# A two-layer 2D state-space block: near sums, their exponentials and DVE's near powers moved by one step in the first layer's scan

## The chip, the cores and the metric

The kernel runs on one NeuronCore of a Trainium2 chip, as one launch. The metric is the device time of that launch in microseconds (us). The time of a kernel is the median of its runs.

The engines go by short names: PE (TensorE, the matrix products; PEld is its loading of weights), DVE (VectorE), ACT (ScalarE), POOL (GpSimd) and SP (SyncE, which here issues nearly all DMAs). Each engine works through its own instructions in program order. An instruction that waits holds up everything behind it on its engine.

## The reference, cut to what matters

The input is a batch of 4 images of 64x64 positions with 192 channels. Two layers of a selective state-space model (four scan directions, 384 inner channels, 16 states) are added to it one after the other. Only the first layer's scan is touched by the change:

```
x = x + layer0(groupnorm(x))
x = x + layer1(groupnorm(x))

# layer0, for each of 4 directions, over the 4096 positions in that direction's order
delta = softplus(dts @ W_dt + b)            # 384 channels
h = exp(delta * A) * h + delta * B * u      # h: 384 x 16 states; A = -exp(A_log)
y = sum over the 16 states of h * C         # then + u * D
```

In this data `A` is -1, -2, ..., -16 (up to a common factor) for the 16 states. So the decay for state n is the n-th power of one decay, and the powers can be made one from the other by a product.

## The kernel before, in words

**Blocks and rounds.** The scan of the first layer goes over the 4096 positions in blocks of 30, which makes 137 rounds. A round treats one block of all four directions and all four images at once, in tiles of 128 partitions (two halves of 64 rows; each half has two directions of 30 rows, and 4 rows for the state carried in) and 1536 columns (4 images of 384 channels). Within a round there are 16 steps, one for each state, from state 16 down to state 1. So there are 2192 steps s, each belonging to round s // 16.

**One step.** For step s the kernel needs a tile x(s) of 128 x 1536, made as x(s) = x(s-1) * f, with f the exponential of the running sum of delta; the first of a round is dtu * g instead, with g the 16th power at once. This is `grown` (line 1063). Its columns are shared out: DVE makes the first 512 ("near"; line 1069 for the first of a round, line 1073 for the others), POOL the other 1024 ("far"). Into rows 60 to 63 of each half a DMA then writes the state carried over from the round before (`carry_in`, line 1018, DMA at line 1024). `mix` (line 1075, matrix products at line 1079) multiplies x(s) by a masked matrix b and adds the result to two accumulators in PSUM, j = 0 and 1, eight products each in the profile. After that `weigh` (lines 1084 and 1090; line 962 in the last step of a round) multiplies the accumulators by fd, on DVE, so that the next state's mix can add to them. In odd steps `keep_end` (line 1029) first copies both accumulators on ACT to the tile sx. From sx come two DMAs (`shrink`, tile small), a product on POOL (`settle`, line 1042) with an exponential from ACT (`decay`, line 1039), and the DMA `carry_out`, which stores the states for the next round. In even steps `outer` (line 1053) makes the outer products of B and C on PE, with 8 rows, and `cut_b` (line 1061) masks them on DVE.

So there is a chain: mix(s) on PE, in odd steps the copy on ACT, weigh(s) on DVE, mix(s+1) on PE.

**The order is written out by hand.** A loop over s (lines 1095 to 1131) emits for every s, engine by engine, the instructions of that turn. The offsets say how far ahead of the mix each piece is made. With AHEAD = 6 (line 1000), in the turn of step s:

- SP: shrink(s-1), carry_out(s-5), carry_in(s+4), then planned DMAs
- ACT: the copies of step s if s is odd, decay(s-2), then planned work
- POOL: grown(s+6), settle(s-4), then planned work
- DVE: weigh(s), grown(s+6), cut_b(s+2) if s is even, then planned work
- PE: mix(s+1), planned work, outer(s+4) if s is even

"Planned" work is what a round needs once: its deltas, sums and exponentials. `Round.steps` (line 974) lists it with an offset from the round's first step and an engine. An offset of -7 is the ninth step of the round before, counted from 0 (16 - 7 = 9). All of these matrix products go through one PSUM tile p, which has a single buffer, so each new product into p waits until the one before it has been read. In steps 5 to 14 of each round this tile is used for the next round, and from step 11 on for the one after that:

- step 8: `sums_d(1)` (line 922, products at line 845), read in step 9 by `keep_sums` (line 929, ACT, tile fd)
- step 9: `sums_near` (line 913), one product of 128 x 512, the running sums of the near columns
- step 10: `first_near` (line 916) and `fall_near` (line 920) on ACT read it. The first writes g of the near columns back into p, the second writes f of the near columns to another PSUM tile, f0. DVE's grown for the next round's first step reads g from p (line 1069)
- step 10: a repeated `sums_d(0)` whose result nobody reads (a filler product on PE); two more of these stand in steps 12 and 14
- step 11: `v(0)` (line 854; at line 845 with 26 rows), read in step 12 by `parts` (lines 862 and 863, ACT)
- step 13 and 14: the same for `v(1)` and its parts

`spread` (line 837, ACT) stands in every step; it prepares the tiles cs that outer reads. On SP, a round's results are stored in step 6 (`store_y`), after POOL has added the old ones in step 5 (`add_old`, line 965).

The x tiles have 7 buffers, f0 and p one each, b three.

Of the kernel before, what the change touches and what calls it, by code (L numbers as in the profile page):

```python
# [578 lines left out]
class FirstLayer(Stage):  # L579
# [182 lines left out]
    def scans(self):  # L762
        nc, tc = self.tc.nc, self.tc
        with ExitStack() as ctx:
# [44 lines left out]
            class Round:  # L809
# [164 lines left out]
                def steps(self):  # L974

                    s = lambda f, *a: (lambda: f(*a))
                    r = [(-30, "sp", self.load_xd), (-20, "sp", self.load_u), (-12, "sp", self.load_bc)]
                    for i in range(NS // PART):
                        r += [(PART * i - 8 + b, "act", s(self.spread, i, b)) for b in range(NB)]
                    for j in range(2):  # L980
                        r += [(2 * j - 21, "pe", s(self.v, j)), (2 * j - 20, "act", s(self.parts, j))]
                        r += [(2 * j - 19, "act", s(self.exp, j))]
                        r += [(2 * j - 13, "dve", s(self.times_u, j)), (2 * j - 13, "act", s(self.keep_dt, j))]
                        r += [(2 * j - 10, "pe", s(self.sums_d, j)), (2 * j - 9, "act", s(self.keep_sums, j))]
                    r += [(at, "pe", s(self.delta, 0, i)) for i, at in enumerate((-17, -16, -15, -14))]
                    r += [(at, "pe", s(self.delta, 1, i)) for i, at in enumerate((-13, -13, -12, -12))]
                    r += [(-16, "act", self.plus), (-15, "pool", self.rounded), (-14, "act", self.log)]
                    for i, at in ((1, -10), (2, -8)):
                        r += [(at - 1, "pe", s(self.sums_far, i))]
                        r += [(at, "act", s(self.first_far, i)), (at, "act", s(self.fall_far, i))]  # L990
                    r += [(-7, "pe", self.sums_near), (-6, "act", self.first_near), (-6, "act", self.fall_near)]
                    r += [(-4, "sp", self.keep_total), (-2, "act", self.log_total), (-1, "dve", self.test)]
                    r += [(10, "sp", self.load_y), (NS + 5, "pool", self.add_old), (NS + 6, "sp", self.store_y)]
                    r += [(at, "pe", s(self.sums_d, 0)) for at in (-6, -4, -2)]
                    return r

            w_dt, one, shift, zeros, late = self.w_dt, self.one, self.shift, self.zeros, self.late
# [2 lines left out]
            AHEAD = 6  # L1000
# [7 lines left out]
            def planned(s, engine):  # L1008
                for f in plan.get((s, engine), []):
                    f()  # L1010
# [7 lines left out]
            def carry_in(s):  # L1018
                n = state(s)
                m = (n - 1) // 2  # L1020
                v = carry[:, n % 2, m : m + 2].rearrange("c m q r f -> r (m q) c f")
                for r in range(2):
                    to = xs[s][r * HALF + 2 * RW : (r + 1) * HALF].rearrange("q (c f) -> q c f", c=2)
                    nc.sync.dma_start(to, v[r])

            def keep_end(s, j):
                if j == 0:
                    sxs[s] = p3.tile([128, W], F32, name="sx")
                nc.scalar.copy(paired(sxs[s], j), accs[j][:, :, :DI])  # L1029

            def shrink(s):
                small[s] = p3.tile([128, SMALL], F32, name="small")
                for c in range(2):
                    narrow(small[s], sxs[s], c)

            def decay(s):
                back[s] = p3.tile([128, SMALL], F32, name="back")
                n = state(s)
                nc.scalar.activation(back[s], of(s).tot, AF.Exp, bias=late[:, n // 2 : n // 2 + 1], scale=float(n))  # L1039

            def settle(s):
                nc.gpsimd.tensor_tensor(back[s], back[s], small[s], ALU.mult)  # L1042

            def carry_out(s):
                nc.sync.dma_start(carry_of(carry, (state(s) - 1) // 2), back[s])

            def outer(s):
                outs[s] = ps_o.tile([128, LC], F32, name="o")
                cs, p = of(s).cs[s % NS // PART], of(s).r % 2
                for h in range(2):  # L1050
                    n = state(s) - 1 - h
                    at = slice(h * NB * HALF, (h + 1) * NB * HALF)
                    nc.tensor.matmul(  # L1053
                        outs[s][:, at], at_b[p][:, n, :], cs[:, n % PART].rearrange("q b l -> q (b l)"),
                        start=True, stop=True, skip_group_check=True,
                    )

            def cut_b(s):
                bs[s] = p_b.tile([128, 2, NB, HALF], F32, name="b")
                o = outs[s].rearrange("p (h b l) -> p h b l", h=2, b=NB)  # L1060
                nc.vector.tensor_tensor(bs[s], o, bc(masks, 2, NB), ALU.mult)  # L1061

            def grown(s, engine):
                it = of(s)
                if s not in xs:
                    xs[s] = p_x.tile([128, W], F32, name="x")
                if s % NS == 0:
                    part, g = (slice(0, LC), it.m[:, 1, :]) if engine is nc.vector else (slice(LC, W), it.g)
                    engine.tensor_tensor(xs[s][:, part], it.dtu[:, part], g, ALU.mult)  # L1069
                    return  # L1070
                part = slice(0, LC) if engine is nc.vector else slice(LC, W)
                f = it.f0 if engine is nc.vector else it.f
                engine.tensor_tensor(xs[s][:, part], xs[s - 1][:, part], f, ALU.mult)  # L1073

            def mix(s, j):
                for r in range(2):
                    for c in range(2):
                        b = 2 * c + j
                        nc.tensor.matmul(  # L1079
                            accs[j][half(c), r, :DI], bs[s - s % 2][half(r), s % 2, b, :], xs[s][half(r), cols(b)],  # L1080
                            start=s % NS == 0, stop=state(s) == 1, skip_group_check=True,
                        )

            def weigh(s, j):
                n = state(s)
                if n == 1:
                    of(s).end_y(j)
                    return
                acc = accs[j][:, :, :DI]
                nc.vector.tensor_tensor(acc, acc, paired(of(s).fd, j), ALU.mult)  # L1090

            engines = {e.engine for e in (nc.tensor, nc.scalar, nc.vector, nc.gpsimd, nc.sync)}
            with tc.manual_schedule(engines=engines):
                tc.keep_in_program_order(nc.scalar.preload_act_table_set("natural_log_exp_and_others"))
                for s in range(-LEAD, N + 8):
                    on = lambda q: 0 <= q < N
                    pair = lambda q: on(q) and state(q) % 2 == 1
                    if pair(s - 1):
                        shrink(s - 1)
                    if pair(s - 5):  # L1100
                        carry_out(s - 5)
                    if on(s + AHEAD - 2):
                        carry_in(s + AHEAD - 2)
                    planned(s, "sp")
                    if pair(s):
                        for j in range(2):
                            keep_end(s, j)
                    if pair(s - 2):
                        decay(s - 2)
                    planned(s, "act")  # L1110
                    if on(s + AHEAD):
                        grown(s + AHEAD, nc.gpsimd)
                    if pair(s - 4):
                        settle(s - 4)
                    planned(s, "pool")
                    if on(s):
                        for j in range(2):
                            weigh(s, j)
                    if on(s + AHEAD):
                        grown(s + AHEAD, nc.vector)  # L1120
                    if on(s + 2) and s % 2 == 0:
                        cut_b(s + 2)
                    planned(s, "dve")
                    for j in range(2):
                        if on(s + 1):
                            mix(s + 1, j)
                    planned(s, "pe")
                    if on(s + 4) and s % 2 == 0:
                        outer(s + 4)
# [719 lines left out]
```

## Time and profile before

| | us |
|---|---|
| median of 3 runs | 9214.46 |
| lowest and highest | 9201.74, 9224.96 |
| the profiled execution, its own time | 9238.58 |
| its span, first to last instruction | 9236.7 |
| mean granted TensorE clock | 0.938 |

The profile is of one execution, 24 us above the median. The span has three stages: projections up to 711 us, the first layer's scan to 7469 us, and the rest (the end of the first layer, and the second layer) to 9237 us.

A row of a group or timeline gives the line of the code, the engine, the operation, the tile written and the tiles read, and the time. In brackets stands how long the engine sat idle just before, and what the profile takes as the releaser of that wait; "issue" means that it names none. Consecutive equal instructions of an engine are merged into one row (x2 and so on). The granted clock is the share of full speed that PE was given.

### The profile page before, as it was taken

What the parts mean: (1) busy time and instruction counts of PE and PEld (TensorE: products, weight loads), DVE (VectorE), ACT (ScalarE), POOL (GpSimd) and SP (SyncE); (2) the same over time, 40 slices, a digit from 0 to 9 for tenths busy, and PEclk for the clock granted to TensorE, in tenths of its full rate; (3) what the DMA queues carried; (4) which work ended last, traced back from release to release, by engine and by line L of the source; (5) the groups of instructions that cost most, each with busy time, mean ns of one, the idle gap of its engine ahead of it and who ended that gap; (6) DMA issues with size and microseconds to landing.
All of it is one profiled execution on the core that took longest, in us unless ns stands there. A gap on an engine that the chain in (4) does not pass through costs nothing. (4 is left out here: it accounts for less than half of the span.)

```text
span 9236.7 us, 194062 instructions
## 1 busy us (share of the span) xinstructions
PE 8325.8 (90%) x64280; PEld 3607.3 (39%) x64280; DVE 7548.9 (82%) x10238; ACT 6071.9 (66%) x10104; POOL 6605.4 (72%) x3814
## 2 busy tenths in 40 slices
PE   8989999999999999999999999999999945887668
PEld 4433333333333333333333333333333324543457
DVE  3428999999899899898899999999999954796756
ACT  3336676776667667666677767766767745675668
POOL 0008999999999999889999999999999952001460
PEclk9989999999999999999999999999999977887788
DMA  6652322322322322223333333333333379433458
GB/s 186 208 175 65 77 72 72 77 73 71 76 73 74 74 73 74 73 72 81 84 78 81 84 78 81 84 80 79 84 81 80 83 183 249 139 126 121 159 136 292
DMA packets 952264, 971.21 MB, mean 105 GB/s; under 512 B 550176, under 2 KB 802733, under 8 KB 950369
## 3 DMA queue, kind: packets, MB, share of 16 engines
q1 hardware_dynamic: 946192, 951.97, 37.9%
q0 software_dynamic: 5056, 6.66, 0.5%
q8 instruction: 521, 8.54, 0.4%
q14 instruction: 495, 4.05, 0.1%
HBM read 521.83 MB, written 375.80 MB: 97 GB/s over the span
## 5 line engine op out<-in xcount | busy, mean ns | idle before, releaser
L1073 POOL TENSOR_TENSOR x<-x,f 128x1024 f32<-128x1024 f32 x2055 | 4864.3, 2367 | 578.4 <-DMA small<-sx 103.6
L1090 DVE TENSOR_TENSOR acc<-acc,fd 128x768 f32<-128x768 f32 x4110 | 3776.2, 959 | 391.5 <-ACT sx L1029 309.9
L1079 PE MATMUL acc<-x,b 64*64 64x384 f32 x35072 | 3515.9, 511 | 85.7 <-DVE acc L940 78.2
L1029 ACT COPY sx<-acc 128x768 f32<-128x768 f32 x2192 | 1663.7, 807 | 704.2 <-PE acc L1079 618.2
L1079 PEld LDWEIGHTS acc<-x,b 64*64 64x64 f32 x35072 | 1080.6, 134 | 2073.4 <-DVE acc L1090 1493.3
L1073 DVE TENSOR_TENSOR x<-x,f 128x512 f32<-128x512 f32 x2055 | 1392.4, 678 | 0.1
L1053 PE MATMUL o<-cs,at_b 8*128 8x256 f32 x4384 | 1236.4, 401 | 2.0 <-DVE b L1061 2.0
L837 ACT ACTIVATE cs<-at_c,own 8x256 f32<-8x256 f32 x2192 | 1071.0, 495 | 103.3 <-PE o L1053 103.2
L1053 PEld LDWEIGHTS o<-cs,at_b 8*128 8x128 f32 x4384 | 727.4, 184 | 743.4 <-issue 328.3
L845 PE MATMUL p<-dt,steps_f 64*64 64x384 f32 x5480 | 620.9, 525 | 155.6 <-DVE x L1069 107.9
L1061 DVE TENSOR_TENSOR b<-o,masks_f 128x512 f32<-128x512 f32 x1096 | 749.7, 684 | 5.7 <-PE o L1053 5.7
L462 PE MATMUL pp<-xT,w_in 96*128 96x512 f32 x1536 | 705.6, 610 | 21.2 <-ACT pad L1286 20.6
L875 POOL TENSOR_SCALAR d<-l 128x1536 f32<-128x1536 f32 x137 | 201.0, 1467 | 664.9 <-ACT l L871 664.9
L862 ACT ACTIVATE e<-p 128x768 f32<-128x768 f32 x274 | 222.5, 812 | 511.4 <-PE p L845 494.2
L904 ACT ACTIVATE g<-p,shift 128x512 f32<-128x512 f32 x274 | 188.3, 687 | 492.0 <-PE p L899 492.0
L1300 DVE SCALAR_TENSOR_TENSOR acc<-pad,conv_w_s,acc 128x2048 f32<-128x2048 f32 x192 | 440.7, 2345 | 45.3 <-ACT acc L1298 44.1
L965 POOL TENSOR_TENSOR yt<-yt,yold 128x1536 f32<-128x1536 f32 x137 | 471.5, 3441 | 0.0
L1042 POOL TENSOR_TENSOR back<-back,small 128x96 f32<-128x96 f32 x1096 | 425.4, 388 | 14.3 <-DMA small<-sx 9.5
L1039 ACT ACTIVATE back<-tot,late_f 128x96 f32<-128x96 f32 x1096 | 432.3, 395 | 0.3 <-DMA carry<-back 0.3
L462 PEld LDWEIGHTS pp<-xT,w_in 96*128 96x128 f32 x1536 | 288.9, 195 | 365.3 <-issue 336.4
L549 PE MATMUL op<-w_out,v 128*128 128x192 f32 x1536 | 288.1, 345 | 139.7 <-DVE ot L552 101.2
L1281 POOL MEMSET pad<- 128x66 f32 x12 | 1.9, 158 | 547.6 <-DVE acc L1300 446.1
(218 smaller groups left out, 9674.8 us busy)
## 6 DMA issues: line engine op xcount, KB each, us to landing
x<-carry SPq DMA_DIRECT2D x4384, 24.0 KB
ut<-uT SPq DMA_DIRECT2D x548, 180.0 KB
small<-sx SPq DMA_DIRECT2D x2192, 24.0 KB
carry<-back SPq DMA_DIRECT2D x1096, 48.0 KB
zg<-gate SPq DMA_DIRECT2D x64, 768.0 KB
yold<-y_row SPq DMA_DIRECT2D x546, 90.0 KB
y_row<-yt SPq DMA_DIRECT2D x546, 90.0 KB
y_col<-yt SPq DMA_DIRECT2D x546, 90.0 KB
```

The source lines that it names most:

```text
L462: self.tc.nc.tensor.matmul(pp, self.w_in[:, i, e * 128 : (e + 1) * 128], self.xT[:, i, t * LC : (t + 1) * LC], start=(i == 0), stop=(i == ...
L837: nc.scalar.mul(self.cs[part][:, :, b, :], at_c[self.r % 2][:, at : at + PART, :], own[:, b : b + 1])
L845: nc.tensor.matmul(self.m[half(b), a, :DI], w(a, 2 * b + j), t(a, 2 * b + j), start=start and n == 0, stop=stop and n == len(terms) - 1, s ...
L965: nc.gpsimd.tensor_tensor(self.y, self.y, yold, ALU.add)
L1029: nc.scalar.copy(paired(sxs[s], j), accs[j][:, :, :DI])
L1039: nc.scalar.activation(back[s], of(s).tot, AF.Exp, bias=late[:, n // 2 : n // 2 + 1], scale=float(n))
L1053: nc.tensor.matmul(outs[s][:, at], at_b[p][:, n, :], cs[:, n % PART].rearrange("q b l -> q (b l)"), start=True, stop=True, skip_group_chec ...
L1061: nc.vector.tensor_tensor(bs[s], o, bc(masks, 2, NB), ALU.mult)
L1073: engine.tensor_tensor(xs[s][:, part], xs[s - 1][:, part], f, ALU.mult)
L1079: nc.tensor.matmul(accs[j][half(c), r, :DI], bs[s - s % 2][half(r), s % 2, b, :], xs[s][half(r), cols(b)], start=s % NS == 0, stop=state(s ...
L1090: nc.vector.tensor_tensor(acc, acc, paired(of(s).fd, j), ALU.mult)
L1300: nc.vector.scalar_tensor_tensor(acc, part(tap), weight(tap), acc, ALU.mult, ALU.add)
```

## The change

Three edits in the first layer's scan, all of order:

- `sums_near` moves from step 9 (-7) to step 10 (-6) on PE. Its two exponentials move from step 10 to step 11 on ACT. Step 11 is odd, so they now stand behind that step's two copies, its decay and its spread. The filler product of step 10 goes to step 9, where the near sums were; the fillers of steps 12 and 14 stay.
- DVE's part of `grown` is made five steps ahead instead of six. POOL's part stays at six.
- `carry_in` is issued three steps ahead instead of four.

```
-                    r += [(-7, "pe", self.sums_near), (-6, "act", self.first_near), (-6, "act", self.fall_near)]
+                    r += [(-6, "pe", self.sums_near), (-5, "act", self.first_near), (-5, "act", self.fall_near)]
...
-                    r += [(at, "pe", s(self.sums_d, 0)) for at in (-6, -4, -2)]
+                    r += [(at, "pe", s(self.sums_d, 0)) for at in (-7, -4, -2)]
...
-                    if on(s + AHEAD - 2):
-                        carry_in(s + AHEAD - 2)
+                    if on(s + AHEAD - 3):
+                        carry_in(s + AHEAD - 3)
...
-                    if on(s + AHEAD):
-                        grown(s + AHEAD, nc.vector)
+                    if on(s + AHEAD - 1):
+                        grown(s + AHEAD - 1, nc.vector)
```

With that, DVE's product for the next round's first step stands in step 11, behind two weighs that wait for the copies, and v(0), which overwrites p in step 11, is the first PE product that waits for it. Seen as a sequence of forms, the instructions of SP and POOL stand in the same order as before in the steady rounds; the load of carried rows that belonged to step s+1 is now that of step s.

## The prediction

> **What bounds the kernel now.** I first read the page's head and its slices, then the busy time by stretches. The scan of the first layer fills 711 to 7469 us, 73% of the span.
>
> ```profile
> span 9236.7 us, 194062 instructions
> PE 8325.8 (90%) x64280; PEld 3607.3 (39%) x64280; DVE 7548.9 (82%) x10238; ACT 6071.9 (66%) x10104; POOL 6605.4 (72%) x3814
> ```
>
> Columns of the stretches: length, busy time of PE, PEld, DVE, ACT and POOL, then granted clock.
>
> ```profile
> 711.00:7469.00 6758.00, 6472.75 (x56560) 2459.12 (x56552) 6132.92 (x8074) 4711.75 (x8049) 6170.87 (x3556) 0.97 0.31 77
> 1224.28:1272.55 48.27, 46.26 (x421) 17.67 (x414) 44.69 (x61) 34.48 (x59) 45.19 (x27) 1.00 0.31 75
> 2996.30:3047.40 51.10, 49.21 (x422) 18.67 (x414) 45.06 (x61) 34.69 (x59) 45.23 (x27) 0.93 0.30 71
> ```
>
> To see here: one round of 16 steps takes 48.27 us at full clock and 51.1 with the clock at 0.93, for the same instructions. No engine is full; PE, DVE and POOL all come close, so the round is a chain of handovers between PE (mix), ACT (copy), DVE (weigh). Following the DVE's step-6 product from round to round through the trace, of 136 rounds 71 take 48.27 us, 25 take 49.91, 34 take 51.08 and six something else; the mean is 49.39.
>
> Next the timeline of a full-clock round, where the change edits it (start, length, engine, line; idle before it in brackets):
>
> ```profile
> 1236.24 1.12 PE L913 MATMUL p<-dt,steps_f 128*128 128x512 f32 x2
> ...
> 1237.29 1.52 PE L1079 MATMUL acc<-x,b 64*64 64x384 f32 x16
> 1237.40 0.66 ACT L916 ACTIVATE p<-p,shift 128x512 f32<-128x512 f32 x1 [1.37 <-PE p L913]
> ...
> 1238.10 0.66 ACT L920 ACTIVATE f<-p,shift 128x512 f32<-128x512 f32 x1
> 1238.68 1.50 ACT L1029 COPY sx<-acc 128x768 f32<-128x768 f32 x2
> 1238.85 0.69 DVE L1069 TENSOR_TENSOR x<-dtu,p 128x512 f32<-128x512 f32 x1 [1.15 <-issue]
> ...
> 1239.59 0.88 PE L845 MATMUL p<-dt,steps_f 64*64 64x384 f32 x8 [0.78 <-DVE x L1069]
> 1240.06 1.82 DVE L1090 TENSOR_TENSOR acc<-acc,fd 128x768 f32<-128x768 f32 x2
> ...
> 1240.40 1.12 PE L1053 MATMUL o<-cs,at_b 8*128 8x256 f32 x4
> ...
> 1241.45 1.52 PE L1079 MATMUL acc<-x,b 64*64 64x384 f32 x16
> ...
> 1242.90 0.88 PE L845 MATMUL p<-w_dtk_f,xd 26*64 26x384 f32 x8
> ...
> 1243.85 0.81 ACT L862 ACTIVATE e<-p 128x768 f32<-128x768 f32 x1 [1.78 <-PE p L845]
> 1244.55 0.81 ACT L863 ACTIVATE up<-p 128x768 f32<-128x768 f32 x1
> ...
> 1245.24 1.51 ACT L1029 COPY sx<-acc 128x768 f32<-128x768 f32 x2
> ```
>
> Once a round, DVE idles 1.15 us before L1069. L1069 starts 0.09 us after L920 ended (1238.76), not after L916 (1238.06), so it waits for both exponentials. The filler product on PE shares tile p with L916, waits for L1069 and leaves PE empty for 0.78 us; outer (L1053), the next mix, v (26-row L845), its two ACT readings and the copy of step 13 all queue behind that. The last view, of waits over the run (total us, times, longest), says that this is every round:
>
> ```profile
> DVE x L1069 <- issue: 153.1, 133, 1.5
> ...
> PE p L845 <- DVE x L1069: 107.9, 136, 2.2
> ```
>
> The same hole costs clock. In the scan the granted clock falls to half in 62 spells (338 us), each of 3.41 or 6.83 us; nearly all begin 17.4 to 17.8 us after the step-6 product, here 1241.7 to 1242.1. The 3.41 us before each contain the hole and the 8-row outer product. Over full 3.41 us stretches of the scan, PE without outer was busy at most 1.65 us wherever a spell followed in an ordinary round; from 1.88 us up none followed.
>
> **The change part by part.** Times are of the round above. Instructions, their counts and durations stay; only places change.
>
> Filler in step 9 instead of the near sums. It needs the read of fd (L929, ended 1235.64); PE gets there at 1236.24. No wait, and 0.88 us instead of 1.12: the next mix starts at 1237.05 instead of 1237.29, needing only the weigh that ends at 1236.84.
>
> Near sums in step 10. They follow that mix: 1238.50 to 1239.62, overwriting a filler that nobody reads. Outer 1239.55 to 1240.68 (its buffer is freed by L1061, now done at 1238.88), mix of state step 12 at 1240.61 instead of 1241.45. The 0.78 hole is gone from here.
>
> Exponentials in step 11 behind the copies. Where ACT is free, the copy starts 0.90 after its mix (trace: 1255.94, 1256.83): 1237.95 instead of 1238.68. From first copy to the end of decay and spread ACT takes 2.05 us (1238.68 to about 1240.73). So L916 starts at 1240.00, L920 ends at 1241.36. Queued behind them on ACT is one spread, then L862; both have time.
>
> DVE's product in step 11. It goes at 1241.45 behind the two weighs (1238.80 to 1240.63), ends 1242.14. DVE still idles some 0.8 us, but what is queued behind it is the weigh of step 12, whose mix half is ready only at 1241.5: it starts 1242.05 instead of 1242.40.
>
> The wait goes to v(0), next on PE: 1242.19 instead of 1242.90; PE ends mix at 1242.13, so the hole is near 0.1. Then L862 at 1243.14 and the copy of step 13 at 1244.54 instead of 1245.24. Everything after is paced by L863 and this copy, so all of it moves by 0.70 to 0.71. Times 137 rounds: 97 us. With a wait on L916 only it would be 0.85; with v(0) 0.7 later, nothing: these are the ends.
>
> DVE's near powers at five steps: they now end 10 to 12 us before their mix instead of 13 to 15. Covered; POOL's part, in its old place, ends 14 to 17 us before.
>
> Carried rows (SP). Each load goes out a step later, but the sequence of loads on SP stays: the slot that brought step 12's rows brings step 11's. They wait for the DVE product one step later too, which moves with them. SP, not DVE, limits here: the stores of y hold it until 1230.5, and the slot goes out at 1233.26, 3.1 us after its DVE product. Taking each slot's landing from the trace and holding it against the mix one step earlier: step 11 has a median of 0.96 us left, step 10 1.9, all others over 2. With step 11's mix 0.24 earlier, 24 rounds (mostly each third of the first half) come short, by 15 us together, and the middle round some 3 more, partly already in today's wait. I take 13 us lost; ends 0 and 70 (half a microsecond in every round).
>
> Clock. New stretches without the hole: the leanest holds outer, mix and v, 1239.6 to 1243.0, about 2.2 us of PE without outer, above the 1.88 that drew no spell. If 26-row products counted for nothing, it would be about 1.5, but only for stretches starting within 0.1 or 0.2 us of one place. What the spells cost: 25 x 1.64 + 34 x 2.81 = 137 us, and 2 for an odd one: 139. The Trainium skill speaks against this saving: "TensorE: Matmul & The Clock Gate", section "HAM oscillation — how this bites in real kernels", holds that PE-idle gaps above about 3.4 us bring the clock down. By it a 0.78 us hole is harmless, the spells have another cause and stay: 9238.6 - 97 + 13 = 9155. By the rows they stand right behind the hole and go with it: 9016. I take the rows.
>
> Sum: the profiled execution's 9238.6 - 97 - 139 + 13 = 9016. It ran 24 us above the median 9214.5, so about 8992.
>
> **The rivals.**
> - Clock stays as it is, the skill's reading: 9155 - 24 = 9131. For it: the limit lies inside an interval I know only from 1.65 to 1.88. Against: the place of the spells.
> - The chain moves but another engine swallows it: POOL is busy 45.19 of 48.27 us, with gaps some 45.9, against 47.56 wanted; or step 11's rows land 0.5 to 0.7 us late each round. With nothing of the 97 left: 9238.6 - 139 + 13 - 24 = 9089; with half, 9040. Against: POOL still catches up with mix, idling 0.8 us at one place and 1.6 at another; about 0.1 and 0.9 would remain.
> - Slower: the hole only moves in front of v(0). If L920 ended after about 1242.0, 0.6 later than worked out, PE would idle 0.7 us beside outer and v, leaner than today, and two halved windows could follow in each round: 137 x 2.81 = 385 instead of 139, so 9214.5 + 246 - 97 + 13 = 9376. It would need a copy or the near sums to be late; both have a measured duration and no new wait.
> - The change not doing what it says: in both builds the L1069 product carries waits on ACT and POOL; none on the carried rows of the step itself is added.
>
> **How the numbers follow.** Main case 0.76, between about 8955 and 9030. Clock stays 0.10, swallowed 0.07, slower 0.07. A measurement of this kernel can tell about 0.3% (28 us) from no change. The first three cases lie below that bound but for 0.02 (clock stays and the chain is swallowed): faster 0.91, same 0.02, slower 0.07. The range 8955 to 9065 holds the main case and the half-swallowed ones.
>
> **What would show it.** Rounds near 47.55 us instead of 48.27, almost none at 51.1; granted clock of the scan 0.99 or more; the wait of PE's L845 on L1069 down from 0.78 to about 0.1 a round, now at 26-row products; DVE's idle before L1069 still 0.8; copy of step 11 right behind its mix. Wrong if halved clock persists at another place of the round, if PE waits for carried rows in most rounds, or if POOL's idle time vanishes and rounds stay at 48.

## The result, and the profile after

| | before | after |
|---|---|---|
| median of 4 runs (us) | 9217.6 | 9080.0 |
| lowest and highest | 9201.7, 9225.0 | 9064.9, 9099.5 |
| profiled execution, its own time | 9238.6 | 9073.7 |
| its span | 9236.7 | 9071.8 |

The row of before has one run more than the table ahead of the prediction. The ratio is 0.9854, with a 95% interval from 0.983 to 0.9878: the changed kernel is 1.5% faster. The forecast was 8992 with a range up to 9065, so the sign was right and the gain, 138 us, fell short of the 225 forecast. This time lies 15 us above the range.

The stretches of the kernel after (columns as in the prediction): first its whole scan, then a plain round of the first half, a stalled one right behind it, and a round of the second half.

```profile
711.00:7303.70 6592.70, 6394.29 (x56561) 2462.41 (x56561) 6117.93 (x8072) 4692.52 (x8046) 6170.87 (x3555) 1.00 0.32 79
1353.16:1400.76 47.60, 46.50 (x422) 17.65 (x414) 44.66 (x60) 34.42 (x59) 45.17 (x27) 1.00 0.31 76
1400.76:1449.87 49.11, 46.80 (x422) 18.59 (x414) 44.84 (x61) 34.33 (x59) 45.20 (x27) 1.00 0.30 74
5542.76:5591.06 48.30, 46.82 (x421) 18.14 (x414) 44.72 (x61) 34.35 (x59) 45.23 (x27) 1.00 0.33 83
```

To see here: the scan's clock went from 0.97 to 1.00, and the plain round from 48.27 to 47.60 us. But two rounds at full clock, with the same work on every engine, take 49.1 and 48.3. Followed from round to round as in the prediction, 63 of 136 rounds take about 47.6 us; the mean is 48.18.

The timeline of the plain round (128.88 us later than the round shown in the prediction):

```profile
1365.77 1.74 PE L1079 MATMUL acc<-x,b 64*64 64x384 f32 x16
...
1366.79 1.59 ACT L1029 COPY sx<-acc 128x768 f32<-128x768 f32 x2 [1.88 <-PE acc L1079]
...
1367.44 1.13 PE L913 MATMUL p<-dt,steps_f 128*128 128x512 f32 x2
...
1370.36 0.69 DVE L1069 TENSOR_TENSOR x<-dtu,p 128x512 f32<-128x512 f32 x1 [0.85 <-issue]
...
1371.10 0.87 PE L845 MATMUL p<-w_dtk_f,xd 26*64 26x384 f32 x8
...
1372.04 0.81 ACT L862 ACTIVATE e<-p 128x768 f32<-128x768 f32 x1 [1.35 <-PE p L845]
...
1373.44 1.51 ACT L1029 COPY sx<-acc 128x768 f32<-128x768 f32 x2
```

The hole of 0.78 us is gone: v(0), the 26-row product, follows the DVE product after 0.05 us. The copy of step 13 starts at 1373.44, in the old round's time 1244.56, where the forecast had 1244.54 and the kernel before 1245.24. The other places of the walk hold to 0.07 us but for one: the mix of step 11 starts at 1365.77, in the old round's time 1236.89, where the forecast had 1237.05.

The waits over the run that answer to those shown of before (total us, times, longest):

```profile
PEld p L845 <- DVE x L1069: 101.2, 136, 3.8
DVE x L1069 <- issue: 97.8, 116, 1.2
```

Of PE nearly only the weight load now waits for L1069, beside other PE work; the product's own wait, 107.9 us before, is down to 3.4 us in 5 waits. DVE still waits before it, 0.84 us a time.

**Where the rest went.** The same view, restricted to the scan, with DMA as the releaser. Before:

```profile
ACT tot L937 <- DMA tot<-fd: 15.3, 12, 7.0
...
PE acc L1079 <- DMA x<-carry: 1.9, 3, 0.8
```

After:

```profile
ACT tot L937 <- DMA tot<-fd: 79.8, 70, 2.4
...
PE acc L1079 <- DMA x<-carry: 41.4, 71, 6.4
```

Two kinds of transfer now come late: the carried rows of the mix (3 waits before, 71 now, in 59 of the 137 rounds), and the round's totals that `log_total` (line 937) reads on ACT (12 before, 70 now). They leave SP late; they don't take longer to land. From its issue to its last semaphore update (taken here as the landing) a load of rows takes 2.58 us in the median before, 2.64 after. The timeline of the stalled first-half round shows the first:

```profile
1414.95 1.59 PE L1079 MATMUL acc<-x,b 64*64 64x384 f32 x16 [1.08 <-DMA x<-carry]
...
1415.99 1.50 ACT L1029 COPY sx<-acc 128x768 f32<-128x768 f32 x2 [3.48 <-PE acc L1079]
1416.82 1.83 DVE L1090 TENSOR_TENSOR acc<-acc,fd 128x768 f32<-128x768 f32 x2 [1.18 <-ACT sx L1029]
```

The mix of step 11 stands idle for 1.08 us until its rows land, and the copy and the weigh behind it are late by as much. SP's own timeline of that round says why. The durations are those of issuing, not of the transfer:

```profile
1404.58 2.61 SPq L972 DMA_DIRECT2D y_col<-yt  x2
1407.23 0.86 SPq L972 DMA_DIRECT2D y_row<-yt  x2
```

The eight stores of y (`store_y`, of which two pairs are shown) stand ahead of the loads of carried rows on SP. A pair of issues mostly takes 0.85 to 1.0 us; here one pair took 2.61. In the first half an issue of over 1 us comes in 22 of 66 rounds before and in 27 after, in the second half in 13 and 36 of 65. So slow issues are in the kernel before too, where they cost little.

The second half's round, SP first:

```profile
5559.22 1.58 SPq L956 DMA_DIRECT2D yold<-y_col  x2
5560.91 0.59 SPq L1024 DMA_DIRECT2D x<-carry  x2
5561.60 1.17 SPq L1016 DMA_DIRECT2D small<-sx  x2
5562.86 0.56 SPq L1045 DMA_DIRECT2D carry<-back  x1
5563.53 0.90 SPq L1024 DMA_DIRECT2D x<-carry  x2
5564.48 1.17 SPq L1016 DMA_DIRECT2D tot<-fd  x2
```

And what ACT and DVE make of it:

```profile
5568.01 0.28 ACT L937 ACTIVATE tot<-tot 128x96 f32<-128x96 f32 x1 [1.70 <-DMA tot<-fd]
...
5569.58 1.50 ACT L1029 COPY sx<-acc 128x768 f32<-128x768 f32 x2
...
5570.41 1.82 DVE L962 TENSOR_TENSOR yt<-acc,fd 128x768 f32<-128x768 f32 x2 [1.19 <-ACT sx L1029]
```

Loads of old y, rows, shrinks and the totals leave SP one behind the other without a gap. The totals land at 5568.0; ACT has stood 1.70 us for them, with the last copies of the round queued behind, so DVE's last weigh waits 1.19.

**The account.** A step is measured from its first weigh to the next step's; the undisturbed step is the median over all rounds. The excess is what the steps of all rounds but the first have above that.

| us in the scan | before | after | forecast |
|---|---|---|---|
| undisturbed round | 48.27 | 47.60 | 47.55 |
| its gain over the scan | | 91 | 97 |
| spells of halved clock | 62, 338 us | 10, 37.5 us | almost none |
| excess over the undisturbed round | 147 | 79 | 21 (147 - 139 + 13) |
| of it in the first half, in the second | | 16, 62 | |
| of it at step 10 (mix of 11) | | 38 | |
| of it at steps 14, 15, 0 of the second half | | 39 | |

Before, nearly all of the excess is clock. After, at most about 18 of the 79 us are clock (an estimate: 9 x 1.64 + 2.81, by what a spell cost before). Nine of the 10 spells begin in step 15 of second-half rounds, where PE waits. Outside the scan nothing moved (2480.6 and 2479.1 us).

### The profile page after: what moved, and what is told of

Read it like the earlier page. It is cut to its first block, busy times and chain, and to the rows that moved or that the text cites. A ratio compares the mean times of both kernels' runs of the same rounds, so it can differ in the third digit from the quotient of the medians.

```text
span 9071.8 us, 194263 instructions
## 1 busy us (share of the span) xinstructions
PE 8250.5 (91%) x64280; PEld 3615.7 (40%) x64280; DVE 7532.0 (83%) x10238; ACT 6053.4 (67%) x10104; POOL 6608.1 (73%) x3814
## 5 line engine op out<-in xcount | busy, mean ns | idle before, releaser
L845 PE MATMUL p<-dt,steps_f 64*64 64x384 f32 x5480 | 598.1, 505 | 43.2 <-ACT up L863 25.5
```

Of the source, the lines that this page charges most:

```text
L845: nc.tensor.matmul(self.m[half(b), a, :DI], w(a, 2 * b + j), t(a, 2 * b + j), start=start and n == 0, stop=stop and n == len(terms) - 1, s ...
```

## The experiments

**Theory A:** SP's issuing, one queue in a fixed order, makes rows and totals late, since a load issued one step later has no slack left. **Theory B:** the change's own order on PE (a filler in step 9, the sums in step 10) costs what is missing. **Theory C:** the clock explains the gain in another way than by the hole. (In the expectations, B stands for any cause but SP's queue, and C in experiments 9 and 10 for loads that land slowly wherever they stand.) Ratios are to runs of the kernel before beside each experiment, with medians of 9208.0 (1 to 4), 9209.1 (5 to 8) and 9216.3 (9 to 11); brackets hold the 95% intervals.

**1 to 3: other orders on SP, from the kernel after.** In the first, a step's `carry_in` goes ahead of shrink and carry_out; in the second only `load_u` moves; the third does both.

```
+                    if on(s + AHEAD - 3):
+                        carry_in(s + AHEAD - 3)
                     if pair(s - 1):
...
-                    if on(s + AHEAD - 3):
-                        carry_in(s + AHEAD - 3)
...
-                    r = [(-30, "sp", self.load_xd), (-20, "sp", self.load_u), (-12, "sp", self.load_bc)]
+                    r = [(-30, "sp", self.load_xd), (-17, "sp", self.load_u), (-12, "sp", self.load_bc)]
```

> The changed kernel, but in each turn SP issues the load of the carried rows ahead of the shrink and carry_out DMAs, not behind them. Theory A (the shortfall of the change against its forecast is carried rows that leave SP too late: mix of step 11 waits in about every third round, mix of step 0 in the second half): step 11's slot comes 1.2 to 1.8 us earlier, its stall (38 us of excess over the base round in the changed kernel's trace) goes, the one at step 0 stays since there SP is held by the loads of u, not by shrink: 9080 - 35 = about 9045. Theory B (the rest is clock or shared-port time, not the queue): no change, 9080 within 10.

Measured 9270.3, ratio 1.006 [1.0041, 1.0078]: a miss, and on the other side. The waits of SP, from 900 to 7400 us, say why. After:

```profile
SPq L1024 <- DVE x L1073: 144.6, 137, 1.9
```

Rows first:

```profile
SPq L1024 <- DVE x L1073: 486.8, 370, 3.7
```

The load into x must wait for the product that makes x. At the head of the turn that product is not ready; SP stands, and all that is queued behind it with it. ACT's wait for the totals rises to 183.5 us, PE's for rows to 96.5, and 64 clock spells come back. SP's order decides, but the place that the load has, behind shrink, is the better one.

> The changed kernel, but the four loads of u for the next round leave in step 15 instead of step 12 on SP. Theory A: the slot with step 0's rows leaves SP 1.9 us earlier, so the excess of steps 14 and 15 in the second half (33 us, halved-clock spells among it) goes, step 11's stays: about 9050. Theory B: no change.

Measured 9058.7, 0.984 [0.9818, 0.9862]. The interval overlaps with that of the kernel after, so the times alone don't show a gain; the profile does: the scan took 6576.3 us instead of 6594.5. Part of what was expected came: PE's idle time before the first mix of a round went from 19.6 us to 0, and the second half's excess at step 15 from 17 to 3. Step 14 kept 18: the totals there stand behind the loads of old y, not behind these.

> Both edits of the two runs before together. Theory A: both stalls go, nearly every round runs at the base of 47.6 us: 9080 - 65 = about 9015. Theory B: 9080 within 10.

Measured 9210.0, 1.0002 [0.9992, 1.0011]: a miss as the first, and the same wait of SP is long here, 516.2 us.

**4: the rows' edit alone, on the kernel before.**

```
-                    if on(s + AHEAD - 2):
-                        carry_in(s + AHEAD - 2)
+                    if on(s + AHEAD - 3):
+                        carry_in(s + AHEAD - 3)
```

> The kernel before with only the carried rows issued three steps ahead instead of four; sums, exponentials, filler and DVE's powers as before. Theory A: the rows are late for mix of step 11 in about every third round and at step 0 in the second half, some 20 to 60 us slower than before (9217): about 9255, and PE waits for them visibly; the halved-clock spells remain at about 60. Theory B: same time as before.

Measured 9202.7, 0.9983 [0.9969, 0.9996]: a miss of 52 us. Some rows came late (PE idle 12.9 us before the mixes of step 11, 4.2 before those of step 0), far fewer than in the kernel after. The profile has 41 spells against 62 in that of before. But the profiled execution of before ran above its median, with more halved clock than usual, so how much of that fall comes from the moved rows is not settled.

**5: the other half of the change without the moved sums.** Powers five ahead, rows three ahead, but near sums and exponentials in their old places, and no filler in steps 9 and 10. Against the kernel before, beside the edits of powers and rows:

```
-                    r += [(at, "pe", s(self.sums_d, 0)) for at in (-6, -4, -2)]
+                    r += [(at, "pe", s(self.sums_d, 0)) for at in (-4, -2)]
```

> DVE's powers five ahead and carried rows three ahead as in the change, but near sums and exponentials in their old places (steps 9 and 10) and the filler of that place left out altogether. By the walk with measured durations: v(0) at about 1242.0 on the scale of the round at 1224.28 us, 0.2 earlier than forecast for the change, so a base round of about 47.35 us. PE without outer is busy about 1.7 to 1.8 us in the leanest 3.41 us stretch. If the limit for halved clock is near 1.65: almost no spells, about 9050. If it is above 1.8: some spells in half of the rounds, about 9150.

Measured 9250.1, 1.0046 [1.0028, 1.0063]. Neither number came: the undisturbed round fell to 47.87 us only (step 10 took 3.92 us where I had worked out 3.62), and 42 spells with 379 us of halved clock remained. So with the filler out instead of the sums moved, 0.40 of the 0.67 us come, but the clock still falls; the whole gain needs the sums and exponentials one step later. Most spells here followed 3.41 us stretches with PE, outer left out, busy about 1.4 us.

**6 and 7: the fillers.** The first takes the step-9 filler out of the kernel after, the second the step-10 filler out of the kernel before. The first edit; the second takes -6 out of before's (-6, -4, -2) likewise:

```
-                    r += [(at, "pe", s(self.sums_d, 0)) for at in (-7, -4, -2)]
+                    r += [(at, "pe", s(self.sums_d, 0)) for at in (-4, -2)]
```

> The changed kernel without its filler product in step 9. Mix of step 11 can start 0.17 us earlier (limited by weigh), the hole left is 0.55 us beside a full mix (PE without outer over 2 us in any stretch). If the filler is needed for the clock: spells come back, 9150 or more. If only lean stretches below about 1.65 to 1.88 us count: no spells, 9080 less up to 20.

Measured 9082.3, 0.986 [0.9833, 0.9888], as expected. The undisturbed round is 47.6, spells 12 against 10. The moved filler does nothing. The sums in step 10 are tested by experiment 10, which keeps them there and has almost no excess; with that, theory B falls.

> The kernel before without its filler product in step 10. The product that waits for L1069 is gone, so the base round shortens by about 0.2 us (outer now waits for L1061 behind the same DVE wait), but PE has a hole of about 1.4 us there and without outer is busy only 1 us in the leanest stretch. Clock theory: more spells than before's 62, in 60 to 90% of the rounds, 9217 + about 50. Rival (the idle gap has to be near 3.4 us before the clock drops): spells unchanged or none, 9217 - 27 or less.

Measured 9311.0, 1.0095 [1.0067, 1.0123]. The two readings of the clock differ most here, and less PE work made the kernel slower, by twice the 50 us expected. The scan of this kernel by the stretches:

```profile
711.00:7540.00 6829.00, 6467.31 (x55464) 2466.41 (x55456) 6125.02 (x8070) 4719.01 (x8046) 6170.15 (x3555) 0.96 0.31 76
```

1096 products fewer, and the clock falls from 0.97 to 0.96: 77 spells with 601 us of halved clock instead of 62 with 338. The hole before outer is 1.47 us here, 0.78 before. A wider hole beside outer costs clock; theory C falls.

**8: no load of old results in column order** in the second half, from the kernel after. That part of the sum is left out of the result.

```
-                        elif k % 2 == 0 or r >= MIDDLE:
+                        elif k % 2 == 0:
```

> The changed kernel without the loads of the old column-order results in the second half (up to four DMAs a round fewer on SP in step 10; their sum is left out of the result). Theory A (issue time on SP makes step 0's rows late in the second half): excess of steps 14 and 15 in the second half (33 us) falls below 8, step 11's stays: about 9050. Theory B: no change.

Measured 9038.8, 0.9805 [0.9782, 0.9829]. The DMA waits in its scan:

```profile
PE acc L1079 <- DMA x<-carry: 22.1, 26, 5.8
...
ACT tot L937 <- DMA tot<-fd: 0.6, 1, 0.6
```

The totals' wait falls from 79.8 to 0.6 us and the second half's excess at steps 14, 15 and 0 from 39 to 6, all of it right after the middle of the scan, where the one spell left stands. Step 10 keeps its 40 us: another burst on SP, the stores, is ahead of those rows. This experiment moves fewer bytes too, so it can't tell SP's time from the transfers; experiment 10 can.

**9: the stores of y in two groups,** four in step 6 and four in step 9, from the kernel after (with the kernel after itself once more beside it). In 9 to 11 the loop over s ends before the last round's second group, so 4 of 1092 stores are missing and that part of the result is left out; the scan up to its last weigh is not touched by it.

```
-                    r += [... (NS + 6, "sp", self.store_y)]
+                    r += [... (NS + 6, "sp", s(self.store_y, 0)), (NS + 9, "sp", s(self.store_y, 1))]
```

> The changed kernel with the eight stores of y split on SP: four stay in step 6, four go to step 9, behind the slot of step 11's carried rows. Theory A (step 11's rows are late because eight stores, one of them sometimes of 1 to 2 us, stand ahead of them on SP): that slot leaves SP 1.6 us earlier, the 38 us of excess at step 10 fall below 10, the second half's at steps 14 and 15 stays or grows a little: about 9055. Theory C (the rows land late because the memory side is slow, wherever they stand): 9080 within 10.

> The changed kernel itself, unaltered, beside the others on one chip: 9080 within 15, to compare the two versions above with it under the same conditions.

Measured 9067.8, 0.9843 [0.9827, 0.9858], and the kernel after again 9068.5, 0.9846 [0.983, 0.9861]. The times show no gain, though the step that it aimed at was cured: step 10's excess fell from 38 us to 1. The scan in the profiles is 15 us shorter (6575.6 against 6591.0), but the rest, which the edit does not touch, was as much longer in this execution. In the second half the stalls moved on (the mix is line 1081 there):

```profile
ACT tot L937 <- DMA tot<-fd: 98.3, 81, 3.1
...
PE acc L1081 <- DMA x<-carry: 25.2, 56, 1.8
```

The four late stores push the totals back, and the excess at steps 14, 15 and 0 grew from 39 to 56 us.

**10 and 11: SP's load spread over the round.** The stores as in 9, the loads of old y in steps 10 and 14, `load_u` in step 0; on the kernel after, and the same on the kernel before.

```
-                    r += [(10, "sp", self.load_y), ...]
+                    r += [(10, "sp", s(self.load_y, 0)), (14, "sp", s(self.load_y, 1)), ...]
...
-                    r = [... (-20, "sp", self.load_u) ...]
+                    r = [... (-16, "sp", self.load_u) ...]
```

> The split of the stores, and also the loads of the old results split (four DMAs at most in step 10, the rest in step 14) and the loads of u in step 0 instead of step 12. Theory A: no slot of carried rows and no load of the totals is late any more, nearly every round is at the base of 47.6 us, spells below 5: about 9010, which would be the fastest of all versions. Theory C: 9080 within 15.

Measured 9011.3 (9003.8 to 9023.4), 0.9782 [0.9768, 0.9795], as expected, and the shortest time of this study. Its scan by the stretches:

```profile
711.00:7237.20 6526.20, 6358.48 (x56564) 2409.92 (x56556) 6112.29 (x8072) 4699.23 (x8046) 6171.05 (x3555) 1.00 0.32 80
```

But for those 4 stores these are the same DMAs with the same bytes, in another order: no spell is left, the excess over the undisturbed round is 11 us in all, and PE's wait for rows is down to 3.5 us in 8 waits. The totals were expected on time and are not: ACT still waits for them in 33 rounds, 30.0 us together, but that costs only about 5 us, at step 14. So a wait in these lists is not yet lost time.

> The same three moves on SP, made in the kernel before the change. There the carried rows land 4 to 8 us ahead of their mix, so theory A expects nothing beyond the shift of where halved-clock spells fall: 9209 within 20. If SP's order itself were worth something without the change, it would show here as 50 us or more.

Measured 9207.1, 0.9996 [0.9987, 1.0005], as expected: where each load has a step to spare, SP's order is worth nothing. The 57 us that experiment 10 gains over the kernel after are slack that the change used up, not a gain of their own.

## Why the prediction was right in kind and wrong in size

- **The chain, right.** Forecast 0.70 to 0.71 us a round and 97 us; measured 48.27 to 47.60, 0.67 and 91. The walk through one round held to 0.02 us at the copy of step 13.
- **The clock, right but for the late rows.** Forecast 139 us back; the hole's spells are gone, and 10 others, at stalls that the change brought, cost at most about 18. The Trainium skill's limit for gaps ("TensorE: Matmul & The Clock Gate", section "HAM oscillation — how this bites in real kernels", about 3.4 us), read as the only cause, would have kept all 62; here 0.78 us beside an 8-row product drew them, and a wider hole drew 77. The prediction had all spells at 3.41 or 6.83 us; one was 10.24.
- **The carried rows, the step that failed.** The prediction said: "step 11 has a median of 0.96 us left, step 10 1.9, all others over 2", and "I take 13 us lost". With what before had beside the clock, that leaves 21 us of excess; measured are 79, so this term is 58 us short. Where the prediction looked, it was about right: the excess of the first half is 16 us, nearly all at step 10. The other 62 lie in the second half, where SP issues 90 DMAs a round instead of 86. Medians over all rounds hid that half. In the trace of before, step 0's rows have 2.5 us left in the first half and 0.7 in the second (landing at the last semaphore update, held against the mix one step earlier as in the prediction). And the mix was to come 0.7 us earlier, which the prediction had worked out itself and did not take off: that leaves nothing. In the kernel after, counted from the round's mix of step 6 and in the median of the second half, step 0's mix came 0.67 us earlier and its rows 0.72 later. At step 11 the mix came 0.40 us earlier, not 0.24.
- **The totals, not in the sum at all.** They do not carry rows but ride on SP behind them. In the second half before, they landed in the median 0.1 us ahead of the moment when ACT was free for them; after, 1.2 us behind it. Through ACT they hold the last copies of the round.
- **Why SP did not follow.** Rounds became 0.7 us shorter, SP's issuing did not. It took 38.5 us a round in the first half and 40 in the second, 0.78 and 0.81 of the round before, 0.81 and 0.84 after. Experiments 10 and 11 show that it is SP's order: spread out, it takes the excess from 79 us to 11 in the kernel after and is worth nothing in the kernel before. A load of rows takes as long to land there (2.63 us in the median) as in the kernel after.
- **The offset, a smaller term.** The sum was made for the profiled execution, and 24 us taken off because that one ran above its median. The kernel after was profiled 6 us below its median: 30 us. Together 58 + 30 = 88, which is what lies between 8992 and 9080; the 6 us that the chain fell short are made up by small differences in the first round and outside the scan. In the runs of before beside the experiments the time goes with the granted clock (median 9201 at 0.943, 9222 at 0.940; the profiled execution had 0.938). So the 24 us were most likely clock, which the 139 had already taken back; then they were counted twice.
- **The rivals.** The halved gain (9040) and the swallowed one (9089) lie nearest in time, the second by chance, for the 97 us were not swallowed. One of the two mechanisms named there, rows late in each round, is the one found, though in some rounds and at several steps instead of at step 11 in all. The other, POOL, did not bind: with the same POOL work, experiment 10 holds 47.6 us. The move of the hole before v(0) did not come.
- **What was not tried:** the moved sums alone and the moved powers alone with the filler kept, since these parts share tile p. How the 91 us divide between them stays open. Open too is why some issues on SP take 1 to 2.2 us, and why they became more frequent in the second half.

## What to carry to other kernels

An engine that only issues DMAs has a time budget as well: sum its issue durations over one round. Here 81 to 84% of the round was enough for late issues to push the next ones. Before a chain is shortened or a load moved later, hold every load on that queue (not only the one moved, and each half of the work by itself) against its reader in the new, shorter round. If rows come late, the cure is to spread the bursts around them; a fix at one slot moved much of the backlog to the next. And take the offset of a profiled execution off only after asking which term of the sum it belongs to.

## What the runs showed of the hardware that was not expected

- Issuing one DMA takes SP 0.40 us in the median (19 of 20 at most 0.76), and 86 to 90 of them fill 38 to 40 us of a 47.6 us round. Issues of 1 to 2.2 us come in 35 of 131 rounds before and in 63 after.
- The clock fell beside a PE hole of 0.78 us, mostly for 3.41 or 6.83 us, in experiments 5 and 7 also for up to 23.89. In the profiles of the kernels before and after and of experiments 4, 5, 7 and 11, all spells of a scan begin on one grid: divided by 3413.3 ns, their starts leave the same remainder within 6 ns.
- PE's busy time without outer gives no single limit. In the kernel before, 58 stretches of the grid with 1.65 us were followed by a spell and 25 were not; in experiment 7, 49 with 1.35 to 1.45 us drew none.
- Taking idle-filling products out of the kernel before made it 1% slower (9311.0 against 9209.1): 1096 useless products earned more than they cost.
